# A ring of scores, exponentials over pairs of chunks, and light statistics on ScalarE from tile 5 on

## The chip, the cores and the metric

The kernel runs on one core of a Trainium2 chip. A core has a matrix engine (TensorE, PE in the profile; its weight loads are shown apart as PEld), VectorE (DVE), ScalarE (ACT), GpSimd (POOL) and SyncE (SP, which here only starts DMAs). Each engine takes its own instructions in order, and they wait for one another through semaphores. The metric is the time of one execution on the device in microseconds (us); lower is better.

## The reference

Two layers act on 3327 rows of 256 numbers: a graph convolution, a mixture of experts, a graph attention, and last a causal attention with four heads and four experts in each head. Only the last one is touched. Cut to what matters:

```python
sx = einsum('bsh,ndh->bnsd', x, hl_w) + hl_b            # 4 heads, 64 wide
q = einsum('bnsd,neod->bneso', sx, wq)                  # 4 experts a head
k = einsum('bnsd,nod->bnso', sx, wk); v = einsum('bnsd,nod->bnso', sx, wv)
scores = einsum('bnesd,bntd->bnest', q, k) * d ** 0.5 + causal
qkv = einsum('bnest,bntd->bnesd', softmax(scores), v)
gs = softmax(einsum('bnsf,nef->bnse', out, gate_w) + gate_b)   # gates of the experts
mixed = einsum('bnsed,bnse->bnsd', out, gs)
hn = layernorm(mixed + resid)                           # per head, 64 wide
hx = layernorm(fc2(relu(fc1(hn))) + hn)                 # zeros masked
out = hx * softmax(hx @ fgate_w.T)[..., None] + x
```

Before it, x is normalized over its 256 columns.

## The kernel before

Rows are worked in 26 tiles of 128. `heads` (line 925) is the last stage and runs from about 970 us to the end. Its unit of work is a head of a tile (104 units, in order of tiles). As the attention is causal, tile t has t + 1 key tiles; `span` (1097) cuts them into t // 4 + 1 chunks of at most 512 keys, so units of tiles 0-3 have one chunk, of 4-7 two, of 24 and 25 seven: 392 chunks in all, numbered through in `chunks` (1508).

A chunk goes through these steps, all four experts at once:

- `fill` (1104), TensorE: the scores `pqk` of 128 queries by up to 512 keys, one PSUM bank for each expert. PSUM buffers of the tag "b" are four, and the other small matmuls share them.
- `drain` (1119), VectorE: each expert's scores are copied to `sc` in SBUF, and the largest of each row is kept (the last chunk of a unit adds the causal mask). After the unit's last chunk, one reduction makes `anmax`, the negated maximum.
- `weigh` (1145), ScalarE: `exp(sc - max)` in place, one activation for each expert and chunk, whose accumulated row sum goes to the table `den` at the chunk's own column.
- `turn` (1166), VectorE: one transpose by 32 x 32 blocks of all four experts.
- `attend` (1180), TensorE: the product with the values `vr`, which come from DRAM (`values`, 1159) through SP's queue, summed over the unit's chunks in `po`.

After a unit's last chunk, `over` (1199) copies `po` to `ot` by ScalarE, where POOL multiplies with the padding mask; `back` (1219), one iteration later, turns it with TensorE (`ptO`) and ScalarE copies the result to `qkv`. After a tile's fourth head, `tail` (1326) follows for the tile: gates, mixing, norms, two small linear layers, the final gate, the store. `prepare` (977) and `heads_of` (1026) make the next tile's norm, projections, keys and queries. Tails and preparations are generators that advance one step per iteration of the main loop.

The order on each engine is written out by hand: `InOrder` (50) makes every engine issue in the order of the program. In iteration k of the main loop (1565) the order is: drain until `wanted(k)`; attend chunk k; transpose up to chunk k + 2 (k + 1 where `extra` is 0); load values for k + 2; `weigh` for chunk k + 3 (k + 2), for its first two experts; `back` of the unit that ended before; `over` of the one that ends now; a step of preparations and tails (left out in iterations with a `back`, from tile 8 on); `weigh` for the other two experts; the activations that tails left in `lazy`; the next `fill`. For a unit's first chunk all four experts are weighed after `back`, `over`, preparations and tails. `wanted` (1550) lets drains run so far ahead that the whole unit of the chunk to be weighed is drained. `extra` (1545) is 1 for tiles 5 to 23.

The scores `sc` live in nine rotating buffers of the pool `ats` (932), 512 columns for each expert. The queries of the first five tiles, `qts`, take buffers of that pool too.

`LIGHT` (1086) is 16. Tiles below it take some statistics by VectorE: in `prepare` bn_stats instead of two accumulating activations, in `norm4` (1293) one reduction instead of four accumulating copies, and as the gates' softmax `softmax4` (1273) instead of `weights` (1247), whose sums come with the exponentials and whose reciprocals are powers on POOL. `empty` (949) gives copies out of PSUM to ScalarE or VectorE by a running count of the load of each.

Of the kernel before, what the change touches and what calls it, by code (L numbers as in the profile page):

```python
# [12 lines left out]
F32 = mybir.dt.float32  # L13
# [9 lines left out]
P = 128  # L23
# [5 lines left out]
BLK = 512  # L29
# [72 lines left out]
class Net:  # L102
# [822 lines left out]
    def heads(self, xs, vs, out):  # L925
        tc, a = self.tc, self.a
        nc = InOrder(tc)
        Q = 32
        with ExitStack() as ctx:
            one = ctx.enter_context(tc.tile_pool(name="at", bufs=1))  # L930
            self.work = ctx.enter_context(tc.tile_pool(name="atw", bufs=2))
            scp = ctx.enter_context(tc.tile_pool(name="ats", bufs=9))
            vrp = ctx.enter_context(tc.tile_pool(name="atv", bufs=3))
            tl = ctx.enter_context(tc.tile_pool(name="att", bufs=2))
            sm = ctx.enter_context(tc.tile_pool(name="atsm", bufs=4))
# [5 lines left out]
            )  # L941

            kt = one.tile([P, 4, NP], F32, name="kt")


            load = dict(act=0.0, dve=0.0)
# [78 lines left out]

            def heads_of(t, res, sxt, nz=None, v=None):

                if nz is None:
                    nz = self.work.tile([P, 2, P], F32, tag="xn", name="nz", bufs=1)
                    nonzero(nz, sxt)  # L1030
# [17 lines left out]
                yield  # L1048
                if t < AHEAD:

                    qt = scp.tile([P, 4, BLK], F32, tag="sc", name="qts")[:, :, : 2 * P]
                    qt = qt.rearrange("p h (i q) -> p h i q", i=2)
                else:
                    qt = tl.tile([P, 4, 2, P], F32, tag="qt", name="qt")
# [28 lines left out]

            tails, preps, ready = [], [], {}
            AHEAD = 5
            LIGHT = 16

            def later(n, gen):

# [7 lines left out]
            def span(t, g):  # L1097


                n = t // 4 + 1  # L1100
                lo, hi = (t + 1) * g // n, (t + 1) * (g + 1) // n
                return lo, hi - lo
# [15 lines left out]

            def drain(u, g):

                n = span(u["t"], g)[1] * P
                last = g == u["t"] // 4
                if g == 0:
                    u["sc"] = {}
                    u["mx"] = sm.tile([P, 4, 8], F32, tag="mx", name="mx")
                sc = u["sc"][g] = scp.tile([P, 4, BLK], F32, tag="sc", name="sc")
                for e in range(4):
                    s, m = u["pq"][e][:, :n], u["mx"][:, e, g : g + 1]
                    if last:
                        nc.vector.tensor_tensor_reduce(  # L1130
                            sc[:, e, :n], s, mask[:, BLK - n :], 1.0, NEG, ALU.add, ALU.max, m
                        )
                    else:
                        nc.vector.tensor_scalar(
                            sc[:, e, :n], s, 1.0, None, ALU.mult, ALU.max, accum_out=m
                        )
                    load["dve"] += 0.12 + 0.00104 * n
                if last:
                    u["nmax"] = sm.tile([P, 4], F32, tag="nmax", name="anmax")
                    nc.vector.tensor_reduce(  # L1140
                        u["nmax"], u["mx"][:, :, : g + 1], AX.X, ALU.max, negate=True
                    )
                    load["dve"] += 0.2

            def weigh(u, g, experts):

                n = span(u["t"], g)[1] * P
                q = ready[u["t"]]
                if u["h"] == g == 0 and 0 in experts:
                    q["den"] = sm.tile([P, 16, 7], F32, tag="den", name="aden", bufs=3)  # L1150
                for k in experts:
                    e = u["sc"][g][:, k, :n]
                    nc.scalar.activation(
                        e, e, AF.Exp, bias=u["nmax"][:, k : k + 1],
                        accum_out=q["den"][:, 4 * u["h"] + k, g : g + 1],
                    )
                    load["act"] += 0.26 + 0.00088 * n
# [8 lines left out]
            def turn(u, g):  # L1166


                n = span(u["t"], g)[1] * P
                w = u["sc"][g][:, :, :n]  # L1170
                nc.vector.transpose(w, w)
                load["dve"] += 0.1 + 0.00417 * n

# [331 lines left out]
                nc.sync.dma_start(out=out[ts(t, P), :], in_=fo)  # L1505

            units = [dict(t=t, h=h) for t in range(NT) for h in range(4)]
            chunks = [(u, g) for u in units for g in range(u["t"] // 4 + 1)]
            def begin(u):

                t = u["t"]
# [33 lines left out]
            def extra(k):  # L1545

                t = chunks[min(k + 3, len(chunks) - 1)][0]["t"]
                return int(chunks[k][0]["t"] >= 5 and t // 4 + 1 <= 6)
# [9 lines left out]
            drain_to(wanted(0))  # L1558
            for k in range(2):
                values(*chunks[k])  # L1560
                weigh(*chunks[k], range(4))
            turn(*chunks[0])
            fill_next()
            ended, flipped, weighed = None, 1, 2
            for k, (u, g) in enumerate(chunks):
                drain_to(wanted(k))
                attend(u, g)
# [3 lines left out]
                if k + 2 < len(chunks):  # L1571
                    values(*chunks[k + 2])
                rest = []
                while weighed < min(k + 3 + extra(k), len(chunks)):
                    c = chunks[weighed]
                    if c[1]:
                        weigh(*c, range(2))
                    rest.append((*c, range(2 if c[1] else 0, 4)))
                    weighed += 1
                if ended:  # L1580
                    back(ended)
                last = u if g == u["t"] // 4 else None
# [568 lines left out]
```

## Time and profile before

| | |
|---|---|
| Runs | 2841.45, 2846.56, 2846.6 us, median 2846.56 |
| The profiled execution | 2842.88 us, its span 2840.9 us |
| Granted TensorE clock | 0.98 of full speed |
| Heads stage | about 970 to 2841 us |
| Transposes in it | 392, 816.1 us of VectorE, all sizes |
| Exponentials in it | 1568, 1041.4 us of ScalarE without their accumulator reads |

A profile line names an engine, an operation, what it writes and reads (`sc<-pqk`), the shape, and how often. In grouped views the busy time comes first, then the mean of one in ns, then the idle time of the engine just before such instructions and who ended it. In the timeline each row is a start, a duration, an engine and an operation, and in brackets the idle time before it. All instructions carry line 61, which is the helper that keeps them in order, so they are told apart by the tiles they touch. A scalar accumulation shows as two rows, the activation and ACTIVATION_READ_ACCUMULATOR, and neighbours overlap; the distance between starts is what one costs in a row. TensorE shows each of these matmuls as two records.

### The profile page before, as it was taken

To read this page: it belongs to the slowest core of one execution; us is meant where nothing else is said; L and a number is where in the kernel's file an instruction comes from. 1 tells how busy PE (TensorE), PEld (TensorE's weight loads), DVE (VectorE), ACT (ScalarE), POOL (GpSimd) and SP (SyncE) were. 2 spreads that over 40 slices of the span, in tenths; PEclk is the share of its full clock that TensorE was granted. 3 is DMA by queue.
4 is the path that set the end of the run, shared out by engine and by line. 5 is a ranking of instruction groups with operands and counts; after the bars stand their busy time and mean duration, and the time that the engine had idled before them with its cause. 6 is when DMAs were issued, how large, how long until landed. Compare 5 with 4: busy or idle time off the path is not lost.

```text
span 2840.9 us, 124987 instructions
## 1 busy us (share of the span) xinstructions
PE 2653.9 (93%) x53422; PEld 1970.7 (69%) x53422; DVE 2372.1 (83%) x5521; ACT 1790.9 (63%) x5131; POOL 1077.6 (38%) x1565
## 2 busy tenths in 40 slices
PE   7999988878988998999999999999999999999995
PEld 5888887756767776676666666666666666666664
DVE  5202643589999798999999999999999999999996
ACT  6520135555555467877777777777778777776774
POOL 5541644532133148655444333333233322223122
PEclk9999999989999899999999999999999999999998
DMA  9994568656785333434434443444434434444432
GB/s 379 386 339 138 191 212 281 202 188 238 277 285 174 94 91 88 117 109 112 119 108 117 118 116 114 119 120 121 115 115 116 126 116 124 123 117 117 116 106 80
DMA packets 257755, 449.29 MB, mean 158 GB/s; under 512 B 58768, under 2 KB 156176, under 8 KB 257072
## 3 DMA queue, kind: packets, MB, share of 16 engines
q1 hardware_dynamic: 245104, 417.11, 47.0%
q0 software_dynamic: 6576, 18.02, 1.7%
q8 instruction: 420, 6.88, 1.0%
q10 hardware_dynamic: 5520, 6.18, 0.6%
q14 instruction: 135, 1.11, 0.1%
HBM read 392.98 MB, written 25.88 MB: 147 GB/s over the span
## 4 chain that ended last, share of the span: by engine, by line
DVE 35%; PE 30%; ACT 4%; issue 2%; POOL 1%; DMA 0%; POOLq 0%; DVEq 0%; ACTq 0%
DVE sc L61 32%; PE pqk L61 11%; PE po L61 10%; PE acc L61 3%; ACT sc L61 2%; PE ptO L61 2%; PE pq L61 1%; PE psxt L61 1%; DVE p L61 1%; PE ph L61 0%; PE pk L61 0%; PE pt L61 0%; DVE sg L61 0%; ACT sq L61 0%; DVE u L61 0%
## 5 line engine op out<-in xcount | busy, mean ns | idle before, releaser
L61 ACT ACTIVATE sc<-sc,anmax 128x512 f32<-128x512 f32 (+3 forms) x1568 | 1041.4, 669 | 101.9 <-DVE anmax L61 101.8
L61 PEld LDWEIGHTS po<-sc,vr 32*64 32x64 f32 x43728 | 659.2, 131 | 300.9 <-issue 149.1
L61 DVE STREAM_TRANSPOSE sc<-sc 128x2048 f32<-128x2048 f32 (+3 forms) x392 | 816.1, 2082 | 11.7 <-ACT sc L61 11.5
L61 PE MATMUL po<-sc,vr 32*64 32x128 f32 x43728 | 758.8, 275 | 32.4 <-DVE sc L61 18.2
L61 PE MATMUL pqk<-kt,qt 64*128 64x512 f32 (+1 forms) x2944 | 764.8, 586 | 19.4 <-DVE fgs L61 7.1
L61 DVE TENSOR_SCALAR_CACHE_REDUCE sc<-pqk 128x512 f32<-128x512 f32 (+2 forms) x1152 | 653.3, 621 | 28.7 <-PE pqk L61 26.7
L61 PEld LDWEIGHTS pqk<-kt,qt 64*128 64x128 f32 x2944 | 315.0, 186 | 240.7 <-issue 85.5
L61 PE MATMUL acc<-wh,p 128*128 128x259 f32 x1352 | 310.9, 387 | 35.3 <-DVE p L61 35.2
L61 PEld LDWEIGHTS acc<-wh,p 128*128 128x128 f32 x1352 | 254.0, 191 | 92.2 <-DVE p L61 51.9
L61 PE MATMUL acc<-y,pan 128*128 128x256 f32 x1352 | 298.4, 382 | 1.7 <-issue 1.7
L61 ACT ACTIVATION_READ_ACCUMULATOR sc<-sc,anmax 128x1 f32 x1568 | 299.5, 191 | 0.0
L61 PEld LDWEIGHTS acc<-y,pan 128*128 128x128 f32 x1352 | 257.2, 191 | 38.7 <-issue 3.3
L61 POOL TENSOR_TENSOR ot<-ot,sxd 128x512 f32<-128x512 f32 x83 | 105.8, 1275 | 435.9 <-ACT ot L61 435.9
L61 DVE CUSTOM_DVE_ANT_0 sc<-pqk,mask 128x512 f32<-128x512 f32 (+3 forms) x416 | 242.0, 636 | 21.1 <-PE pqk L61 20.8
L61 ACT ACTIVATE u<-u,d 128x512 f32<-128x512 f32 (+1 forms) x182 | 125.1, 688 | 156.4 <-DVE u L61 156.2
L61 DVE SCALAR_TENSOR_TENSOR p<-pan,u 128x512 f32<-128x512 f32 (+1 forms) x182 | 127.7, 702 | 11.7 <-PE acc L61 7.3
L61 DVE SCALAR_TENSOR_TENSOR u<-bc,d 128x512 f32<-128x512 f32 (+1 forms) x182 | 136.3, 749 | 0.1
L61 PE MATMUL ptO<-igw,ot 128*128 128x68 f32 x832 | 116.1, 283 | 4.3 <-DVE sc L61 2.1
L61 ACT COPY qkv<-ptO 128x272 f32<-128x272 f32 x104 | 39.7, 382 | 126.7 <-PE ptO L61 126.6
L61 PEld LDWEIGHTS ptO<-igw,ot 128*128 128x128 f32 x832 | 101.8, 193 | 23.1 <-issue 15.2
L61 ACT ACTIVATE junk<-ar 128x1664 bf16<-128x1664 f32 x52 | 82.8, 1592 | 54.3 <-DMA ar<-in_adj_dram 53.7
L61 DVE CUSTOM_DVE_ANT_0 sg<-sg,dst 128x1664 bf16<-128x1664 bf16 (+2 forms) x56 | 100.7, 1806 | 1.2 <-ACT dst L61 1.0
(366 smaller groups left out, 3074.6 us busy)
## 6 DMA issues: line engine op xcount, KB each, us to landing
vr<-vs SPq DMA_DIRECT2D x976, 128.0 KB
ar<-in_adj_dram SPq DMA_DIRECT2D x104, 832.0 KB
vr<-vs SPq DMA_DIRECT2D x544, 96.0 KB
pan<-in_adjt_dram SPq DMA_DIRECT2D x156, 256.0 KB
pan<-in_adjt_dram SPq DMA_DIRECT2D x26, 1024.0 KB
pan<-in_adjt_dram SPq DMA_DIRECT2D x20, 832.0 KB
w1e<-w SPq DMA_DIRECT2D x59, 256.0 KB
took<-places SPq DMA_DIRECT2D x59, 129.0 KB
```

What stands on the lines that cost most here:

```text
L61: made = make(*args, **kw)
```

## The change

The nine buffers become one tile `ring` of nine slots, with the column of a chunk worked out by hand (six slots for the 24 chunks of tiles 0-4, whose queries lie in the last three). Where an even chunk that is not the unit's last has the next slot beside it (`paired`), it is put at the end of its slot, so that it and the next chunk lie side by side, and one activation for each expert takes the exponential of both and leaves one sum; the second column of `den` is then never written, so the table is zeroed by POOL in `heads_of`, with four buffers instead of three. `weigh` takes the number of a chunk. In the main loop a pair that does not begin a unit is split over two iterations, two experts in each; a pair that begins a unit is weighed whole, after `back`, `over`, preparations and tails. `LIGHT` becomes 5. The lines of the steps `fill`, `attend`, `values`, `turn`, `extra` and `wanted` stay as they are but for the place of the scores.

```diff
@@ -929,7 +929,6 @@
         with ExitStack() as ctx:
             one = ctx.enter_context(tc.tile_pool(name="at", bufs=1))
             self.work = ctx.enter_context(tc.tile_pool(name="atw", bufs=2))
-            scp = ctx.enter_context(tc.tile_pool(name="ats", bufs=9))
             vrp = ctx.enter_context(tc.tile_pool(name="atv", bufs=3))
             tl = ctx.enter_context(tc.tile_pool(name="att", bufs=2))
             sm = ctx.enter_context(tc.tile_pool(name="atsm", bufs=4))
@@ -941,6 +940,10 @@
             )
 
             kt = one.tile([P, 4, NP], F32, name="kt")
+
+
+            RING = 9
+            ring = one.tile([P, 4, RING * BLK], F32, name="ring")
 
 
             load = dict(act=0.0, dve=0.0)
@@ -1025,6 +1028,9 @@
 
             def heads_of(t, res, sxt, nz=None, v=None):
 
+                den = sm.tile([P, 16, 7], F32, tag="den", name="aden", bufs=4)
+                nc.gpsimd.memset(den, 0.0)
+                res.update(den=den)
                 if nz is None:
                     nz = self.work.tile([P, 2, P], F32, tag="xn", name="nz", bufs=1)
                     nonzero(nz, sxt)
@@ -1048,7 +1054,7 @@
                 yield
                 if t < AHEAD:
 
-                    qt = scp.tile([P, 4, BLK], F32, tag="sc", name="qts")[:, :, : 2 * P]
+                    qt = ring[:, :, ds(6 * BLK + 2 * P * t, 2 * P)]
                     qt = qt.rearrange("p h (i q) -> p h i q", i=2)
                 else:
                     qt = tl.tile([P, 4, 2, P], F32, tag="qt", name="qt")
@@ -1083,7 +1089,7 @@
 
             tails, preps, ready = [], [], {}
             AHEAD = 5
-            LIGHT = 16
+            LIGHT = 5
 
             def later(n, gen):
 
@@ -1118,12 +1124,15 @@
 
             def drain(u, g):
 
+                c = u["c"] + g
                 n = span(u["t"], g)[1] * P
+                at = slot(c) * BLK + (BLK - n if paired(c) else 0)
                 last = g == u["t"] // 4
                 if g == 0:
-                    u["sc"] = {}
+                    u["sc"], u["at"] = {}, {}
                     u["mx"] = sm.tile([P, 4, 8], F32, tag="mx", name="mx")
-                sc = u["sc"][g] = scp.tile([P, 4, BLK], F32, tag="sc", name="sc")
+                sc = u["sc"][g] = ring[:, :, ds(at, n)]
+                u["at"][g] = at
                 for e in range(4):
                     s, m = u["pq"][e][:, :n], u["mx"][:, e, g : g + 1]
                     if last:
@@ -1142,14 +1151,24 @@
                     )
                     load["dve"] += 0.2
 
-            def weigh(u, g, experts):
-
+            def slot(c):
+
+                return c % (RING if c >= 24 else 6)
+
+            def paired(c):
+
+                u, g = chunks[c]
+                return g % 2 == 0 and g < u["t"] // 4 and slot(c) + 1 == slot(c + 1)
+
+            def weigh(c, experts):
+
+                u, g = chunks[c]
                 n = span(u["t"], g)[1] * P
+                if paired(c):
+                    n += span(u["t"], g + 1)[1] * P
                 q = ready[u["t"]]
-                if u["h"] == g == 0 and 0 in experts:
-                    q["den"] = sm.tile([P, 16, 7], F32, tag="den", name="aden", bufs=3)
                 for k in experts:
-                    e = u["sc"][g][:, k, :n]
+                    e = ring[:, k, ds(u["at"][g], n)]
                     nc.scalar.activation(
                         e, e, AF.Exp, bias=u["nmax"][:, k : k + 1],
                         accum_out=q["den"][:, 4 * u["h"] + k, g : g + 1],
@@ -1167,7 +1186,7 @@
 
 
                 n = span(u["t"], g)[1] * P
-                w = u["sc"][g][:, :, :n]
+                w = u["sc"][g]
                 nc.vector.transpose(w, w)
                 load["dve"] += 0.1 + 0.00417 * n
 
@@ -1505,7 +1524,11 @@
                 nc.sync.dma_start(out=out[ts(t, P), :], in_=fo)
 
             units = [dict(t=t, h=h) for t in range(NT) for h in range(4)]
-            chunks = [(u, g) for u in units for g in range(u["t"] // 4 + 1)]
+            chunks = []
+            for u in units:
+                u["c"] = len(chunks)
+                chunks += [(u, g) for g in range(u["t"] // 4 + 1)]
+
             def begin(u):
 
                 t = u["t"]
@@ -1558,10 +1581,10 @@
             drain_to(wanted(0))
             for k in range(2):
                 values(*chunks[k])
-                weigh(*chunks[k], range(4))
+                weigh(k, range(4))
             turn(*chunks[0])
             fill_next()
-            ended, flipped, weighed = None, 1, 2
+            ended, flipped, weighed, begun = None, 1, 2, 0
             for k, (u, g) in enumerate(chunks):
                 drain_to(wanted(k))
                 attend(u, g)
@@ -1571,12 +1594,21 @@
                 if k + 2 < len(chunks):
                     values(*chunks[k + 2])
                 rest = []
-                while weighed < min(k + 3 + extra(k), len(chunks)):
-                    c = chunks[weighed]
-                    if c[1]:
-                        weigh(*c, range(2))
-                    rest.append((*c, range(2 if c[1] else 0, 4)))
-                    weighed += 1
+                until = min(k + 3 + extra(k), len(chunks))
+                while weighed < until:
+                    left = range(begun, 4)
+                    if chunks[weighed][1]:
+                        half = len(left) // 2
+                        weigh(weighed, left[:half])
+                        left = left[half:]
+                    rest.append((weighed, left))
+                    weighed += 2 if paired(weighed) else 1
+                    begun = 0
+                if weighed < len(chunks) and chunks[weighed][1] and paired(weighed) and not begun:
+                    if not rest or rest[0][1][0] > 1:
+                        weigh(weighed, range(1))
+                        rest.append((weighed, range(1, 2)))
+                        begun = 2
                 if ended:
                     back(ended)
                 last = u if g == u["t"] // 4 else None
```

## The prediction

> **What bounds the kernel now.** I read the page first, then the busy times by stretch, the chain of waits, VectorE's waits, and the timeline around single units. The page's busy shares and the chain that ended last:
>
> ```profile
> PE 2653.9 (93%) x53422; PEld 1970.7 (69%) x53422; DVE 2372.1 (83%) x5521; ACT 1790.9 (63%) x5131; POOL 1077.6 (38%) x1565
> ...
> DVE 35%; PE 30%; ACT 4%; issue 2%; POOL 1%; DMA 0%; POOLq 0%; DVEq 0%; ACTq 0%
> ```
>
> VectorE and TensorE share the end; ScalarE carries 4% of the chain. The shares are means, so here are the stretches of the heads stage: tiles 5-7, 8-11, 12-15, 16-23, 24-25 (a tile starts with its first transpose). Columns: window, length, then busy us and instructions of PE, weight loads, DVE, ACT, POOL.
>
> ```profile
> 1102.00:1229.90 127.90, 124.04 (x2944) 88.33 (x2928) 116.54 (x299) 96.72 (x309) 89.03 (x123) 0.99 0.38 108
> 1229.90:1460.10 230.20, 226.09 (x5908) 157.56 (x5914) 218.50 (x531) 173.69 (x546) 115.05 (x155) 1.00 0.40 113
> 1460.10:1762.10 302.00, 295.19 (x8138) 203.57 (x8130) 292.11 (x670) 222.55 (x689) 120.25 (x165) 0.99 0.41 116
> 1762.10:2571.10 809.00, 797.00 (x22870) 539.50 (x22861) 794.17 (x1710) 610.19 (x1934) 243.79 (x336) 1.00 0.41 119
> 2571.10:2841.00 269.90, 222.44 (x7030) 150.80 (x7013) 243.97 (x539) 177.19 (x565) 62.55 (x86) 0.97 0.36 104
> ```
>
> VectorE is busy 91, 95, 97 and 98% in the first four. TensorE's figure holds stalls inside its matmuls, so I take its floor from unstalled pieces of the chain: scores of a chunk 1.49 us (384 wide) or 1.92 (512), its attention 1.58 or 2.02, 1.04 per unit for the way back, some 6.15 per tile for projections and tail. Tile 10 (chunks 384, 512, 512): 4 x (5.33 + 5.62 + 1.04) + 6.15 = 54.1 us, against 56.9 of VectorE. So VectorE sets the pace from tile 8, by a little at first, alone from tile 12. Its waits from 1100 to 2700 us:
>
> ```profile
> DVE sc L61 <- PE pqk L61: 38.2, 45, 4.9
> DVE sc L61 <- ACT sc L61: 0.9, 3, 0.4
> ```
>
> It almost never waits for exponentials: 0.9 us. That is the cover the change draws on. One unit (tile 20, head 3):
>
> ```profile
> 2206.90 0.18 DVE L61 TENSOR_REDUCE anmax<-mx 128x4 f32<-128x24 f32 x1
> 2207.00 2.30 DVE L61 STREAM_TRANSPOSE sc<-sc 128x2048 f32<-128x2048 f32 x1
> 2207.12 0.62 ACT L61 ACTIVATE sc<-sc,anmax 128x384 f32<-128x384 f32 x1 [2.62 <-DVE anmax L61]
> ...
> 2208.93 0.60 ACT L61 ACTIVATE sc<-sc,anmax 128x384 f32<-128x384 f32 x1
> ...
> 2209.44 0.18 ACT L61 ACTIVATION_READ_ACCUMULATOR sc<-sc,anmax 128x1 f32 x1
> 2209.53 0.70 ACT L61 ACTIVATE sc<-sc,anmax 128x512 f32<-128x512 f32 x1
> ...
> 2211.11 1.77 DVE L61 STREAM_TRANSPOSE sc<-sc 128x1536 f32<-128x1536 f32 x1
> ```
>
> The exponentials of a unit's first chunk cannot start before its maximum (2207.08), and VectorE comes to their transpose 4.03 us later, after one other transpose and one drain. Four exponentials of 384 take 4 x 0.60 = 2.41; they are done at 2209.62, so 1.49 us are spare.
>
> **The change, part by part.** *Paired exponentials.* Starts are 0.60 us apart at 384 columns and 0.705 at 512, so 0.00082 us per column and 0.28 fixed. A pair drops one fixed part for each of four experts. Of 168 candidate pairs in tiles 4-25 the ring's wrap cuts 18: 150 x 4 x 0.28 = 168 us less ScalarE work. But all four double exponentials of a unit's first pair stand before the first transpose. In the unit shown, 4 x 1.02 (896 columns) = 4.08, plus the 0.12 that the last read and the signal take: 2207.12 + 4.20 = 2211.32 against 2211.11, a new wait of 0.21 us on VectorE. Queued behind it are that transpose and the next chunk's drain, whose score banks TensorE's next fill wants; the attention of the chunk itself comes two iterations later and has slack.
>
> The wait is larger where the start is late:
>
> ```profile
> 2128.07 0.37 ACT L61 COPY xt<-pt 128x256 f32<-128x256 f32 x1 [8.90 <-PE pt L61]
> 2128.34 0.62 ACT L61 ACTIVATE sc<-sc,anmax 128x384 f32<-128x384 f32 x1
> ```
>
> Here (tile 20, head 0) a copy of the next tile's preparation, in line before the exponentials, waited for TensorE, and they started 2.5 us after the maximum. The change leaves that order. I took start and transpose of all 81 units whose first chunk pairs and put in the longer exponentials (1.02 us at 896 columns, 1.13 at 1024, less for shorter): waits add up to 2.5 us in tile 4, 6.1 in 5-7, 11.6 in 8-11, 6.5 in 12-15, 15.1 in 16-23, 4.0 in 24-25, 45.8 in all. Were every start immediate (0.03 us after the maximum), it would be 11.5. These are the two bounds. Late starts come mostly from TensorE's order, which stays, so I keep the upper one but count 0.8 of the 25.6 from tile 12 on (VectorE's chain; some of its waits for scores shrink in return) and 0.4 of the 20.2 before (TensorE nearly equal): 20.5 + 8.1 = **+28.6**.
>
> The row and a page differ here. The Trainium skill (ScalarE: Activation LUTs, What ACT_TABLE_LOAD costs) gives 280 ns + 0.833 per column, with 93 ns of overlap back to back, and names no accumulator read; by it four of 896 would last 3.73 us, and the 0.21 above would vanish, the change coming out as in the first rival. The 0.60 and 0.705 measured here include the accumulator read, and I go by them.
>
> *Statistics from tile 5 on.* VectorE loses, per tile, by its rows: the sums l1ns and l2ns 0.32 + 0.30, bn_stats, aggregate and epsilon 0.32 + 0.19 + 0.15, and in the gates a subtraction, two sums and two reciprocals, 0.17 + 0.15 + 0.12 + 0.18 + 0.16; with 0.02 between dependent ones some 2.25 us, 24.7 over 11 tiles. It counts until TensorE's floor: in 5-7 the floors sum to 115.1 against 116.5, so 1.4; in 8-11 209.5 against 218.5, all 9.0; in 12-15 all 9.0. That is 19.4 at best; two nearly equal engines never meet exactly, so **-17** (bounds -10, -19.4). ScalarE gains per tile eight sums at 0.36, four gate exponentials at 0.28 for one of 0.2, and two statistics of some 0.5 and 0.6: 5.0 us, 55 in all. From tile 16 on these run today, and the xres reader there shows no idle before it, so the load is not late. In 5-7, with 10 pairs, ScalarE grows by 15 - 11.3 = 3.7 on 96.7 of 127.9 us. That is room on the mean; bursts can still hold a copy that TensorE wants. Bounds 0 and +6, taken **+1**, as tiles 16-23 carry the same bursts with VectorE at 98%. POOL gains two powers (1.02, 0.57) and two small multiplies, 2.0 us a tile, with 39 us idle in 5-7; without that room it would be 22 us.
>
> A rule speaks against this part: the same page (Rules for kernel authors) sends additions to VectorE, not ScalarE. The rows agree on cost, 0.32 against 4 x 0.36; by the rule the 55 us given to ScalarE outweigh 24.7 and the part would lose some 30 us. It would where ScalarE was the bound, which the stretches deny.
>
> *Less ScalarE work elsewhere.* 168 - 55 = 113 us net. The chain holds ScalarE for 4%, mostly bursts before a copy that TensorE's next fill wants; what can come back is part of the 38.2 us above. Bounds 0 and -10, taken **-4**.
>
> *Ring, zeroed sums, query tiles.* No DMA moves. A slot is nine chunks behind from chunk 24, as the buffers were; earlier six serve where a drain runs at most four ahead. The transposes already step over gaps (1.77 us for 384 columns, 2.30 for 512: the slope of the data alone). The zeroing is one POOL write per tile; the nearest row, 256 columns, takes 1.08 us, 26 x 1.08 = 28 us at most, all inside POOL's idle time and a tile ahead of its reader. **0** for all; if a slot were late on the first tiles, some 2 us.
>
> Sum: 28.6 - 17 + 1 - 4 = **+8.6 us**. The profiled execution took 2842.88 us (span 2840.9 and 2 around it), 3.7 under the median of the runs, 2846.56; on the median it makes 2855, on the profile 2851. I say **2854**.
>
> **Rivals.** *VectorE's relief wins.* If ScalarE, with 113 us less to do, is ready at each maximum, the wait is 11.5 at most, about 8 exposed: 8 - 17 - 4 = -13, 2834. For it: three units in four from tile 16 start within 0.1 us already. Against it: the late ones wait for TensorE. It decides below an exposed wait of 15 us. *They cancel.* With about 20 us exposed the sum is 0: 2847. *ScalarE's bursts become the bound in tiles 5-15.* There VectorE's relief is worth nothing and each of 11 tiles loses 2 us more behind the sums: 8.6 + 17 + 22 = +48, 2894; half of it 2870. Against it, the mean load under 80%. *The ring does not do what it says*: if slices of the one tile were taken to overlap, each of the 150 pairs would hold back a drain of another slot, at 1 us each +150. The key table kt is one tile written and read by slices today, and its writes wait only for their own matmuls.
>
> **How the numbers follow.** Slower by the unit's wait 0.38 (own range 2849 to 2866); relief wins 0.32; cancel 0.17; bursts 0.11; ring 0.02. A measurement of this kernel tells about 0.2%, 5.7 us, from no change. Faster 0.32, same 0.17, slower 0.51. The range 2831 to 2876 leaves out the low end of the relief and the high end of the bursts.
>
> **What would show it.** VectorE's waits for "ACT sc" grow from 0.9 to 20-45 us, at first transposes of units; ScalarE's exponentials fall by 600, its busy time by 100 us or so; tiles 16-25 become 10 to 18 us longer and 5-15 a few us shorter or equal. Wrong, if those waits stay under 10 us, or if tiles 16-25 keep their length.

## The result and the profile after

The changed kernel takes 2911.88 us in the median (2907.19 to 2917.77, five runs), the kernel before 2846.60 beside it (2841.45 to 2849.00): 1.023 times as long, 95% interval 1.0214 to 1.0246, or 65 us more. The prediction said 2854 with a range up to 2876: the right direction, an eighth of the size.

The page of the changed kernel, busy shares and the chain that ended last:

```profile
PE 2683.9 (92%) x53422; PEld 1984.8 (68%) x53422; DVE 2357.5 (81%) x5411; ACT 1671.6 (57%) x4239; POOL 1104.1 (38%) x1635
...
PE 28%; DVE 24%; ACT 15%; POOL 3%; issue 2%; SPq 1%; DMA 0%; POOLq 0%; DVEq 0%; ACTq 0%
```

ScalarE works 119 us less than before (1790.9) and yet its share of the chain goes from 4% to 15%. VectorE, 15 us less busy, falls from 35% to 24%. Work became less and waiting became more. The same stretches as before, by tiles 5-7, 8-11, 12-15, 16-23, 24-25 (window, length, then busy us and instructions of PE, weight loads, DVE, ACT, POOL):

```profile
1103.80:1240.80 137.00, 125.91 (x2900) 89.59 (x2902) 113.74 (x280) 93.35 (x274) 92.44 (x133) 0.98 0.36 101
1240.80:1484.80 244.00, 231.11 (x5932) 159.83 (x5931) 211.69 (x489) 176.27 (x542) 119.65 (x168) 0.99 0.38 106
1484.80:1798.60 313.80, 301.49 (x8118) 202.82 (x8116) 286.52 (x634) 207.56 (x572) 134.82 (x193) 0.99 0.40 112
1798.60:2634.00 835.40, 809.02 (x22874) 545.73 (x22870) 795.03 (x1698) 535.67 (x1399) 247.55 (x347) 0.99 0.41 115
2634.00:2910.00 276.00, 224.69 (x6970) 152.67 (x6962) 244.60 (x537) 151.81 (x397) 62.77 (x87) 0.95 0.36 101
```

They are longer by 9.1, 13.8, 11.8, 26.4 and 6.1 us: about half of the loss lies in tiles 5-15, where the prediction had "a few us shorter or equal"; tiles 16-25 lose 32.5 us where it had 10 to 18. In tiles 16-23 VectorE does the same work (795.0 us against 794.2) in 26.4 us more. VectorE's waits from 1100 to 2770 us (us in total, times, longest):

```profile
DVE ring L61 <- PE pqk L61: 66.3, 66, 6.2
DVE ring L61 <- ACT ring L61: 50.6, 61, 2.1
```

The wait for exponentials grew from 0.9 to 50.6 us; that for scores from 38.2 to 66.3, of which the prediction expected some to shrink. (Its other signs came: 600 exponentials fewer and some 100 us less of ScalarE; the wait was put at 20 to 45.) The unit shown of before (tile 20, head 3), in the timeline of after:

```profile
2262.43 0.18 DVE L61 TENSOR_REDUCE anmax<-mx 128x4 f32<-128x24 f32 x1
2262.52 2.30 DVE L61 STREAM_TRANSPOSE ring<-ring 128x2048 f32<-128x2048 f32 x1
2262.64 1.04 ACT L61 ACTIVATE ring<-ring,anmax 128x896 f32<-128x896 f32 x1 [4.04 <-DVE anmax L61]
...
2265.73 1.03 ACT L61 ACTIVATE ring<-ring,anmax 128x896 f32<-128x896 f32 x1
...
2266.67 0.19 ACT L61 ACTIVATION_READ_ACCUMULATOR ring<-ring,anmax 128x1 f32 x1
...
2266.89 1.78 DVE L61 STREAM_TRANSPOSE ring<-ring 128x1536 f32<-128x1536 f32 x1 [0.17 <-ACT ring L61]
```

Four exponentials 1.03 us apart, 4.25 us from the first start to the transpose, and a wait of 0.17 us: the prediction worked out 0.21 for this unit. So the picture of the wait is right. What it is worth, and what else was lost, is what the experiments are for.

### The profile page after: what moved, and what is told of

Its sections match the earlier page's. It is cut to its first block, busy times and chain, and to the rows that moved or that the text cites. A ratio compares the mean times of both kernels' runs of the same rounds, so it can differ in the third digit from the quotient of the medians.

```text
span 2910.0 us, 124041 instructions
## 1 busy us (share of the span) xinstructions
PE 2683.9 (92%) x53422; PEld 1984.8 (68%) x53422; DVE 2357.5 (81%) x5411; ACT 1671.6 (57%) x4239; POOL 1104.1 (38%) x1635
## 4 chain that ended last, share of the span: by engine, by line
PE 28%; DVE 24%; ACT 15%; POOL 3%; issue 2%; SPq 1%; DMA 0%; POOLq 0%; DVEq 0%; ACTq 0%
DVE ring L61 21%; ACT ring L61 11%; PE po L61 10%; PE pqk L61 9%; PE acc L61 4%; PE ptO L61 2%; ACT sq L61 1%; POOL fx L61 1%; PE pq L61 1%; SPq L61 1%; PE psxt L61 1%; PE ph L61 1%; DVE p L61 0%; PE pt L61 0%; DVE sg L61 0%
## 5 line engine op out<-in xcount | busy, mean ns | idle before, releaser
L61 ACT ACTIVATE ring<-ring,anmax 128x896 f32<-128x896 f32 (+7 forms) x968 | 873.5, 907 | 146.4 <-DVE anmax L61 146.3
L61 PEld LDWEIGHTS po<-ring,vr 32*64 32x64 f32 x43728 | 670.9, 132 | 301.1 <-issue 132.5
L61 DVE STREAM_TRANSPOSE ring<-ring 128x2048 f32<-128x2048 f32 (+3 forms) x392 | 816.2, 2083 | 66.8 <-ACT ring L61 66.3
L61 PE MATMUL pqk<-kt,qt 64*128 64x512 f32 (+1 forms) x2944 | 779.1, 589 | 51.9 <-ACT qt L61 11.5
L61 PE MATMUL po<-ring,vr 32*64 32x128 f32 x43728 | 770.3, 278 | 31.1 <-DVE ring L61 17.9
L61 DVE TENSOR_SCALAR_CACHE_REDUCE ring<-pqk 128x512 f32<-128x512 f32 (+2 forms) x1152 | 653.8, 621 | 47.5 <-PE pqk L61 46.1
L61 PE MATMUL acc<-wh,p 128*128 128x259 f32 x1352 | 309.9, 386 | 36.5 <-DVE p L61 36.4
L61 DVE CUSTOM_DVE_ANT_0 ring<-pqk,mask 128x512 f32<-128x512 f32 (+3 forms) x416 | 242.2, 636 | 33.1 <-PE pqk L61 32.7
L61 ACT ACTIVATION_READ_ACCUMULATOR ring<-ring,anmax 128x1 f32 x968 | 185.2, 191 | 0.0
L61 PEld LDWEIGHTS ptO<-igw,ot 128*128 128x128 f32 x832 | 102.1, 193 | 30.4 <-issue 13.0
```

The source lines that it names most:

```text
L61: made = make(*args, **kw)
```

## The experiments

Edits are against the changed kernel unless "before" is said, and all of these but late_first_light put `LIGHT` back to 16. "Whole" means that the block of the main loop that begins a pair an iteration early is taken out:

```diff
-                if weighed < len(chunks) and chunks[weighed][1] and paired(weighed) and not begun:
-                    if not rest or rest[0][1][0] > 1:
-                        weigh(weighed, range(1))
-                        rest.append((weighed, range(1, 2)))
-                        begun = 2
```

Medians in us, each beside the kernel before on the same chip; the waits between 1100 and 2750 us are VectorE's for exponentials and for scores (before: 0.9 and 38.2, to 2700) and, last, TensorE's for ScalarE's other work, nearly all copies, summed over its tiles (before: 5.1). The waits are those of the profiled execution; for odd_pairs that is its shortest run (2884.1), for odd_whole its longest (2870.2).

| run | this | before | ratio, 95% interval | waits: ACT, PE pqk | TensorE for ACT |
|---|---|---|---|---|---|
| ring_only | 2846.91 | 2845.85 | 0.9997 (0.9986 to 1.0008) | 0.6, 38.8 | 5.1 |
| pairs_only | 2899.07 | 2845.85 | 1.0190 (1.0168 to 1.0212) | 36.5, 47.7 | 22.3 |
| light_only | 2857.46 | 2845.85 | 1.0044 (1.0029 to 1.0058) | 2.1, 65.2 | 15.3 |
| odd_pairs | 2895.27 | 2845.85 | 1.0176 (1.0159 to 1.0193) | 9.2, 63.3 | 38.5 |
| odd_whole | 2859.58 | 2849.65 | 1.0036 (1.0022 to 1.0051) | 3.3, 50.9 | 10.6 |
| even2_whole | 2857.23 | 2849.65 | 1.0029 (1.0018 to 1.0040) | 2.6, 40.2 | 9.8 |
| even_whole | 2880.51 | 2843.76 | 1.0115 (1.0078 to 1.0151) | 37.2, 34.7 | 8.0 |
| first_only | 2882.95 | 2843.76 | 1.0132 (1.0096 to 1.0168) | 36.6, 35.7 | 7.9 |
| half_first | 2854.53 | 2848.55 | 1.0028 (1.0015 to 1.0040) | 5.0, 36.9 | 8.2 |
| single_in_turn | 2984.03 | 2848.64 | 1.0488 (1.0458 to 1.0518) | 2.3, 146.4 | 87.5 |
| odd_over_first | 2876.89 | 2849.65 | 1.0104 (1.0087 to 1.0121) | 25.0, 35.3 | 12.4 |
| before_over_first | 2847.24 | 2849.65 | 0.9997 (0.9983 to 1.0011) | 3.2, 36.6 | 2.8 |
| late_turn | 2897.33 | 2848.64 | 1.0175 (1.0150 to 1.0199) | 2.1, 71.3 | 14.6 |
| late_first | 2888.16 | 2847.33 | 1.0148 (1.0131 to 1.0165) | 1.6, 62.8 | 5.6 |
| late_first_light | 2898.07 | 2847.33 | 1.0174 (1.0157 to 1.0191) | 2.9, 93.8 | 14.2 |
| light_sums | 2855.61 | 2848.64 | 1.0023 (1.0010 to 1.0036) | 0.6, 48.4 | 9.9 |
| light_rest | 2850.05 | 2848.64 | 1.0006 (0.9996 to 1.0015) | 0.8, 55.7 | 9.6 |
| light_26 | 2868.53 | 2848.55 | 1.0076 (1.0063 to 1.0090) | 0.6, 37.3 | 3.5 |

### The parts alone

The ring and the zeroed table without pairs (ring_only), with pairs (pairs_only), and the statistics in the kernel before (light_only):

```diff
ring_only:
-                return g % 2 == 0 and g < u["t"] // 4 and slot(c) + 1 == slot(c + 1)
+                return False and g < u["t"] // 4 and slot(c) + 1 == slot(c + 1)
light_only, before:
-            LIGHT = 16
+            LIGHT = 5
```

> The changed kernel without any pair and with LIGHT back at 16: ring, zeroed table and query tiles alone. First-pair theory (pairs that begin a unit cost the time) and statistics theory (light statistics from tile 5 on cost it): both say as before, 2847 within 4 us, VectorE's waits for exponentials near 1 us. Ring theory (slices of one tile wait for one another): well above 2847, 2870 or more.

> The changed kernel with LIGHT back at 16: ring and pairs. First-pair theory: tiles 16-25 keep the 33 us that the changed kernel is longer there, tiles 4-15 add some 15 more of waits for the first pair, so 2885 to 2900, and with the relief that the statistics were meant to give missing even 2912 or more. Statistics theory: only the 33 us of tiles 16-25 remain, 2880. Ring theory: as the ring alone.

> The kernel before with LIGHT at 5, nothing else. By the recorded step (VectorE's relief counts): 2847 - 17 + 1 = 2831. Statistics theory: slower, 2847 + 15 to 35 = 2862 to 2882, all of it in tiles 5-15, with ScalarE and POOL in the chain there.

The ring costs nothing. Pairs cost 53 us and the statistics 12; together 65, the whole loss: as far as these runs can tell, the two add up. The statistics, from which the prediction hoped for 17 us of gain, lose, though less than the 15 to 35 us of the rival expectation.

### Which pairs cost

If the wait at a unit's first transpose is the cause, pairs that start at the second chunk should be free (odd_pairs). They were not: the excess is 49 us, more than either expectation had (6 at most, or 0.7 of 53):

```diff
-                return g % 2 == 0 and g < u["t"] // 4 and slot(c) + 1 == slot(c + 1)
+                return g % 2 == 1 and g < u["t"] // 4 and slot(c) + 1 == slot(c + 1)
```

> LIGHT 16, and pairs begin at odd chunks (1 and 2, 3 and 4, 5 and 6), so a unit's first chunk is never paired; some 107 pairs remain of 150. First-pair theory: VectorE's waits for exponentials fall back to a few us and the time to 2847 within 6 us, lower if anything. If pairs cost wherever they stand (longer single instructions ahead of the copies): 0.7 of what pairs_only loses.

VectorE's wait for exponentials is almost gone (9.2 us), but its wait for scores stands at 63.3, and TensorE waits for ScalarE's copies (12.2 us for `ot`, 5.6 for `sxt`, 4.7 for `sx`). So there is a second cost, which does not come from first pairs. The suspicion fell on the pairs that are begun early. By the kernel's loop, of the 69 pairs of the change that do not begin a unit 53 are begun one iteration before a single chunk in their place would be, and 16 two or three; of the 113 pairs of odd_pairs 45 are begun early, 41 of them by two. odd_whole takes that away; even2_whole has only the pairs (2, 3) and (4, 5), whole; even_whole all the pairs of the change, whole; first_only the first pair of each unit alone:

```diff
even2_whole:
-                return g % 2 == 0 and g < u["t"] // 4 and slot(c) + 1 == slot(c + 1)
+                return g % 2 == 0 and g and g < u["t"] // 4 and slot(c) + 1 == slot(c + 1)
first_only:
-                return g % 2 == 0 and g < u["t"] // 4 and slot(c) + 1 == slot(c + 1)
+                return g == 0 and g < u["t"] // 4 and slot(c) + 1 == slot(c + 1)
```

> odd_pairs without the splitting of a pair over two iterations. Queue theory: what costs, beside the wait at a first transpose, is the time of exponentials that ScalarE has in line between a unit's maximum and the copy of the previous unit's sums (ot), which TensorE's next attention waits for. Per unit of tiles 16-23, at 512 columns: before 4 + 4 + 2 singles = 7.1 us; odd_pairs 4 singles, 4 and 1 doubles = 8.5; single_in_turn 8 + 4 + 2 singles = 9.9. Here 4 singles and 4 doubles = 7.3, so most of the 29 us that odd_pairs loses in tiles 16-23 comes back: 2850 to 2862. If longer single instructions cost by themselves, it stays at 2885 or more.

> Pairs only from chunk 2 on (2 and 3, 4 and 5), not split over iterations. Queue theory: 4 + 4 singles and 2 doubles stand before ot = 8.0 us, 0.9 more than before, in all units from tile 12: slower than odd_whole, 2865 to 2885. If only first pairs and split pairs cost: 2847 within 6.

> pairs_only without the splitting of pairs over two iterations: first pairs stay. If the splitting is what costs (odd_pairs fell from +50 to +10 without it), 2855 to 2865. If first pairs cost their wait whole, 36 us by VectorE's waits in pairs_only, on top of the 8 that whole pairs from chunk 2 on cost: 2885 to 2893, and the waits for exponentials stay at 30 to 40 us.

> Only the 81 first pairs, chunks 0 and 1, whole; all later chunks single. Wait theory: the 36 to 41 us of waits remain and are all exposed, 2880 to 2890. If they hide in other idle time (the recorded prediction counted 0.4 of them in tiles 4-11 and 0.8 later), 2847 + 8 + 17 = 2872 or less; if splitting alone costs, 2847 within 6.

Each beside its own kernel before, whole pairs cost 39 us less than begun ones in odd_whole (10 against 49), and 16 us less in even_whole (37 against 53; by the ratios 21, give or take 12): beginning a pair early costs that much. TensorE's waits for ScalarE's copies go the same way, from 38.5 to 10.6 us and from 22.3 to 8.0. Pairs later in a unit, kept whole, cost 8 to 10 us (even2_whole, odd_whole; less for the former than the queue theory expected). First pairs alone cost 39 us, all pairs whole 37, which falls between the two expectations for even_whole. In first_only that stands beside a wait of 36.6 us that the kernel before did not have, with VectorE's wait for scores nearly unchanged.

Two numbers alike are no proof that the wait is the cost; late_first, below, takes the wait away and gains nothing. So half_first shortens the wait and leaves the order as it is: in first_only, the first chunk's transpose is done in two halves of two experts, the first of which needs only two of the four exponentials.

```diff
-                nc.vector.transpose(w, w)
+                for h in range(2 if not g and paired(u["c"]) else 1):
+                    x = w[:, ds(2 * h, 2), :] if not g and paired(u["c"]) else w
+                    nc.vector.transpose(x, x)
```

> Only the first pairs of units, whole, as in first_only (36.6 us of VectorE waits for ScalarE, +37 us, about 2883), and the transpose of a paired first chunk is done in two halves of two experts, 81 transposes more. By the slope of the rows (1.77 us for 384 columns, 2.30 for 512) a half costs about 0.2 us of fixed part, so VectorE gets about 16 us more work. Theory: the wait of VectorE for the last of the four double exponentials is itself the cost. The second half is due 1.1 us later than the whole transpose was, most of the 53 waits of 0.7 us mean vanish: waits for ScalarE under 12 us, time 2883 - 28 + 16 = about 2871 (2862 to 2877). Rival: the wait is only where VectorE happens to stand when something else is late (scores, copies); then the waits for ScalarE fall but those for TensorE grow by as much, and the time is 2883 to 2899.

VectorE's waits of first_only, and then of half_first:

```profile
DVE ring L61 <- ACT ring L61: 36.6, 53, 2.1
DVE ring L61 <- PE pqk L61: 35.7, 35, 6.2
```

```profile
DVE ring L61 <- PE pqk L61: 36.9, 42, 6.2
DVE ring L61 <- ACT ring L61: 5.0, 12, 0.9
```

31.6 us of the wait are gone and did not turn up at the scores; the profiled spans went from 2879.3 to 2852.9 us, 26.4 less. The 1.0132 of the first pairs becomes 1.0028, and 2854.5 us is below the 2862 to 2877 expected, because the halves cost less than the 16 us put in for them: 59 chunks of 384 columns take 110.0 us in halves and 104.6 (59 at 1.773) whole, and VectorE's busy time grows by 4.0 us in all. With these, 30.4 of the 31.6 us are accounted for. That the wait for the last of the four exponentials was the price of the first pairs is shown.

### The order on ScalarE

single_in_turn keeps the places and the times at which pairs_only issues a pair, but issues it as eight single exponentials, chunk by chunk; work and instructions are those of ring_only:

```diff
-                n = span(u["t"], g)[1] * P
-                if paired(c):
-                    n += span(u["t"], g + 1)[1] * P
+                for i in range(2 if paired(c) else 1):
+                    u, g = chunks[c + i]
+                    n = span(u["t"], g)[1] * P
...
```

> LIGHT 16, the places and the order of the pairs, but each pair as eight single exponentials, the first chunk's four ahead of the second's. ScalarE has the 170 us more again, and the same clumping, but a unit's first chunk is ready as early as before. Turn theory (the loss of pairs_only, some 53 us, is VectorE standing at the first transpose, 41 us by its trace): VectorE's waits for exponentials fall under 10 us and the time to 2855, within 8. Copy theory (exponentials done earlier than needed stand before the copies that free score banks): 2885 or more, above all in tiles 16-25.

It takes some 135 us more than ring_only for the same instructions in another order: VectorE waits 2.3 us for exponentials, but 146 for scores, and TensorE 87.5 us for ScalarE's copies. A piece of its chain of waits (start, length, engine and tile, pieces joined):

```profile
2005.69 5.32 ACT ring L61 x16
2011.02 0.25 ACT sq L61 x2
...
2012.40 1.41 ACT ring L61 x4
2013.81 0.52 ACT sxt L61 x2
2014.32 0.04 issue
2014.37 1.25 PE pqk L61 x2
2015.62 3.40 PE po L61 x116
```

Here both chunks' exponentials of a unit's first pair (16 rows with their accumulator reads) run first, though the second chunk's are wanted later; then statistics, two exponentials of the next pair, begun early, and only then the copy `sxt`, for which the next scores wait. The chain of the changed kernel has a place of the same kind:

```profile
2007.74 1.08 ACT qt L61 x2
2008.82 0.26 ACT fot L61
2009.09 4.09 ACT ring L61 x8
2013.18 1.12 ACT gss L61 x8
2014.30 1.13 ACT ring L61 x2
2015.43 0.27 ACT sx L61
2015.69 0.04 issue
2015.74 1.31 PE pqk L61 x4
```

Its timeline (cut) names the blocks:

```profile
2008.96 1.06 ACT L61 ACTIVATE ring<-ring,anmax 128x896 f32<-128x896 f32 x1
...
2012.00 0.44 PE L61 MATMUL pt<-ident,sxt 128*128 128x128 f32 x2
...
2014.20 1.14 ACT L61 ACTIVATE ring<-ring,anmax 128x1024 f32<-128x1024 f32 x1
...
2015.74 1.31 PE L61 MATMUL pqk<-kt,qt 64*128 64x512 f32 x4 [1.89 <-ACT sx L61]
```

The copy `sx` of 0.27 us stands behind 6.34 us of exponentials and gate sums: the four of a unit's first pair (896 columns each), the gates' `gss`, and one of 1024 columns, the first expert of the next pair, begun an iteration early. What it copies came from TensorE at 2012.00 to 2012.44, and TensorE waited 1.89 us for it. A doubled exponential is cheaper as a sum, but it is a longer block in a line that is worked in order.

If copies are what suffers, they may go first. odd_over_first puts all exponentials of an iteration behind the copies of `back` and `over` and of preparations and tails; before_over_first does it in the kernel before:

```diff
before_over_first, before:
-                    if c[1]:
-                        weigh(*c, range(2))
-                    rest.append((*c, range(2 if c[1] else 0, 4)))
+                    rest.append((*c, range(4)))
```

> odd_pairs, split as there, but no exponential is issued before the copies qkv and ot of its own iteration; all come after. Queue theory: the double that stood before ot is behind it, 7.3 us again, so 2850 to 2865. If the copies of preparations and tails are what is held, no gain: 2885 or more.

> The kernel before with that order alone: all four exponentials of a chunk after the copies of its iteration. Queue theory: 5.7 us before ot instead of 7.1, so no slower, 2847 within 4, and perhaps some us faster in tiles 5-11. Against it: VectorE's transposes may now wait for the two exponentials that come later, 2850 to 2860.

For the pairs it helps by some 20 us against odd_pairs (27 us over its kernel before, against 49), less than the queue theory expected (2850 to 2865): TensorE's waits for copies fall from 38.5 to 12.4 us and VectorE's for scores from 63.3 to 35.3, but that for exponentials rises from 9.2 to 25.0. The copies' loss is in part handed on to the transposes. Two things changed at once, though: by the loop, the 41 pairs begun two iterations early are here begun only one early, so how much the order alone is worth is not shown. In the kernel before, with single exponentials, the order makes no difference that can be told.

### Transposing later

The first chunk's transpose may come one iteration later, when its exponentials are surely done; late_turn does this for every chunk of tiles 5 to 23, late_first only for first chunks that pair (whole pairs), late_first_light adds `LIGHT` 5:

```diff
late_turn:
-                while flipped < min(k + 2 + extra(k), weighed, len(chunks)):
+                while flipped < min(k + 2, weighed, len(chunks)):
late_first:
+                    if extra(k) and flipped == k + 2 and not chunks[flipped][1] and paired(flipped):
+                        break
```

> LIGHT 16 and all pairs, but transposes run one iteration later in tiles 5-23, so the pair has some 5 us more. Turn theory: VectorE's waits for exponentials in tiles 5-23 fall from 38 to under 5 us; time 2855 within 10, or under 2847 if ScalarE's lighter load then counts. Copy theory: 2885 or more, with the lost time as waits for scores. A third way: TensorE now waits for the late transposes, PE po behind DVE ring, and gives it back.

> even_whole (all pairs, whole, LIGHT 16), only that the transpose of a unit's first chunk is put off by one iteration where it is paired, behind the next drain. Wait theory: the 37 us of waits for exponentials go, the order on ScalarE stays, so 2847 + 0 to 10 us, what whole pairs cost elsewhere; below 2847 only if ScalarE's 170 us less count for anything. If the late transposes hold TensorE, as all late ones did, 2875 or more and PE po waits for DVE ring.

> The same with LIGHT at 5. If the statistics cost 12 us only because ScalarE's line was full, its 170 us less pay for that and VectorE's relief counts: up to 17 us under late_first, so this would be below the kernel before. If the sums stand before the copies all the same: 8 to 14 us over late_first.

None is clearly shorter than its like without the move (late_turn 2897 to pairs_only's 2899, late_first 2888 to even_whole's 2881). The wait theory's times (2855, 2847 to 2857) were missed; what came is the other outcome named, that late transposes hold TensorE. VectorE hardly waits for exponentials any more, but late_turn makes TensorE's attention wait 44.0 us for VectorE's `ring` (9.1 in pairs_only), and late_first makes TensorE wait 17.2 us (`ptO`) and 10.6 (`pqk`) for it (2.0 and 7.8 in even_whole), and VectorE 62.8 for scores. A place in late_first's timeline shows how:

```profile
2167.60 0.69 DVE L61 TENSOR_SCALAR_CACHE_REDUCE ring<-pqk 128x512 f32<-128x512 f32 x1 [2.50 <-PE pqk L61]
...
2170.15 3.97 DVE L61 STREAM_TRANSPOSE ring<-ring 128x1536 f32<-128x1536 f32 x2
```

In the slot that the transpose left, VectorE has nothing to do until scores come (2.50 us); an iteration later it does two transposes in a row (3.97 us), and the drains behind them free the score banks late. With the statistics as well it is another 10 us, within the 8 to 14 expected.

### The statistics

light_sums gives ScalarE only the two norms' sums from tile 5 on, light_rest the other half, gates and the preparation's statistics (both in the kernel before). light_26 goes the other way: all statistics to VectorE up to the last tile.

```diff
light_sums, before (the same for "l2"):
-                yield from norm4(fx, lng, lnb, "l1", t < LIGHT)
+                yield from norm4(fx, lng, lnb, "l1", t < 5)
light_26, before:
-            LIGHT = 16
+            LIGHT = 26
```

> The kernel before, only the two norms' sums by ScalarE from tile 5 on. light_only lost 12 us. Lazy theory (a norm's sums stand in ScalarE's line right before the copy of ptO that TensorE's next scores wait for): most of the loss is here, 2847 + 8 to 14. Statistics-of-rows theory (POOL waits in its order for ScalarE's row statistics and gates, and holds ot back): within 4 us of 2847.

> The kernel before, only the row statistics and the gates moved from tile 5 on, the norms' sums left at 16. It takes 1.6 us of VectorE a tile for 2.1 us of ScalarE. Lazy theory: 2847 or some us less (relief counts: -5 to -10). Statistics-of-rows theory: 2847 + 8 to 12.

> The kernel before with the limit LIGHT at 26 in place of 16: in tiles 16 to 25 the two norms' sums, the gates' sums and reciprocals and the preparation's statistics go to VectorE, which is 98% busy there. By the rows of the prediction 2.25 us of VectorE per tile, 10 tiles: +22 us if VectorE alone sets the pace there (about 2869, tiles 16 to 25 longer by 20 or so). Rival: the end passes to and fro between VectorE and the copies of ScalarE that free score banks, and ScalarE, relieved of 5 us a tile, makes copies sooner: +12 or less (2847 to 2859).

The sums make up some 7 of the 12 us; the rest cannot be told from nothing, though it takes 12 us of work from VectorE, which would have gained time if VectorE set the pace there. A few us of the 12 lie in neither half, or in the noise. The chain of light_only in tile 8 shows their way to the end:

```profile
1228.72 2.39 ACT sc L61 x8
1231.11 0.25 ACT sq L61 x2
...
1233.95 0.44 ACT sq L61 x2
1234.39 1.20 ACT sc L61 x4
1235.59 0.28 ACT qkv L61
1235.86 0.04 issue
1235.91 1.64 PE pqk L61 x2
```

Eight accumulating activations of two norms, 3.3 us, run between the exponentials; the copy `qkv`, 0.28 us, comes last, and TensorE's scores wait for it. Between the starts of tiles 5 and 16 VectorE waits for scores 24.9 us in the kernel before and 47.6 in light_only:

```profile
DVE sc L61 <- PE pqk L61: 24.9, 24, 4.9
```

```profile
DVE sc L61 <- PE pqk L61: 47.6, 57, 4.2
```

VectorE's busy time fell by 18.1 us and its wait for scores rose by 22.7: the relief was turned into waiting. TensorE's waits for ScalarE's copies rose from 5.1 to 15.3 us. light_26 shows that the price itself was right where VectorE alone sets the end: 2.25 us a tile over ten tiles make 22, measured 20 to 22 (1.0076 of 2848.55 is 21.6). There the chain reads

```profile
DVE 42%; PE 25%; issue 2%; ACT 2%; DMA 1%; POOL 1%; SPq 0%; POOLq 0%; DVEq 0%; ACTq 0%
```

with VectorE's share up from 35%. Of the three limits tried, 5, 16 and 26, 16 is the best, and no version here is faster than the kernel before.

## Why the prediction was wrong, by its steps

The prediction fell 56 us short, +8.6 against +65. The step that failed most is the statistics' relief: -16 with its bursts, measured +12, so 28 us. The pairs begun early, at nothing in the sum, are 16; the part of the first-transpose wait that was not counted is 8 or so; the gain from a lighter ScalarE, which did not come, is 4.

| term | predicted | measured |
|---|---|---|
| wait at first transposes | +28.6 | +37 to +39 (even_whole, first_only; 33 to 38 by the ratios) |
| pairs begun early | not in the sum | +16 (pairs_only less even_whole) |
| statistics' relief, with its bursts | -17 + 1 | +12 (light_only) |
| less ScalarE work elsewhere | -4 | no gain: half_first, 90 us of ScalarE less, is 1.0028 |
| ring, zeroing, query tiles | 0 | 0 (ring_only) |

**The wait at first transposes** was seen, and its raw size of 45.8 us was near: 36.5 us in pairs_only, 50.6 in the change, where the statistics delay the exponentials further. What failed is the share of it that was counted, 0.8 from tile 12 on and 0.4 before. The argument was that waits for scores shrink in return, and that TensorE is nearly equal before tile 12. They hardly shrink (35.7 in first_only against 38.7 in the same stretch of before). Practically all of the wait counted, as half_first shows. The reading offered for this, argued and not measured apart: when VectorE waits, the score banks are emptied later too, and two engines that are both nearly full and feed each other through four buffers are not two floors of which the higher one counts.

**The pairs that are split over two iterations** were named in the description of the change and never costed; some are even begun two iterations ahead. That they issue earlier than the single exponentials did was the one thing to see: for every instruction moved forward in an engine's line, ask what it is now in front of. Here it is in front of the copies `ot`, `sx`, `sxt`, `qkv` and `qt`.

**The statistics' relief** was worked out by floors: VectorE's time until TensorE's sum. The size of the edit was right (light_26), but the end in tiles 5-15 does not follow the higher of two floors. The trace of before had shown it: followed stage by stage, its chain gives VectorE 7% in tiles 5-7 and 26% in 8-11, TensorE 69% in both, and VectorE leads only from tile 12 (62%), while the prediction let VectorE set the pace from tile 8. light_rest agrees: 12 us less of VectorE, no time. And the bursts, bounded at 6 us for three tiles because "tiles 16-23 carry the same bursts", cost in tiles 5-15 more than VectorE gained. The rule which the prediction weighed and set aside, that additions belong to VectorE and not to ScalarE (the Trainium skill, ScalarE: Activation LUTs, Rules for kernel authors), had the sign right (light_only, 1.0044). ScalarE was not full, 57 to 64% busy; in the places looked at, what lost was the copies that stood behind the sums in its line. The rival "ScalarE's bursts become the bound in tiles 5-15" had this mechanism, at twice the size for the statistics.

**Less ScalarE work** is the smallest term, but the idea behind the change. 119 us fewer on an engine with idle time gave nothing back that shows, and its share of the chain went up from 4% to 15%. What ScalarE lacked was not time but the right moment.

What stays open: why pairs later in a unit cost 8 to 10 us even when whole (TensorE's waits for copies account for some 5), although with first pairs they add nothing; how the early pairs' 16 us divide between the copies `ot`, `sx`, `sxt`, `qkv` and `qt`; and how late_first's 41 us divide between the emptied slot and the doubled one.

## What to carry to other kernels

Here, fusing small instructions on an engine that works in order and has time to spare saved no time and lengthened the block that stands before the next consumer: before fusing, look at what is waiting for the first half, and what is queued behind the second. A stall between two engines that were both over 90% busy and share few buffers counted in full here, so give no discount on one without a trace that shows the return. If one consumer must wait for a longer block, let it take its input in parts, as the two halves of a transpose did here for 31.6 us of waiting.

## What the runs showed of the hardware that was not expected

TensorE's granted clock fell to half for 3.4 us, at times for 6.8 or 10.2, after stretches in which it did little, and the stalls made by the order on ScalarE were long enough for it. Two neighbouring windows of the changed kernel (length, PE busy and, third from the end, the clock):

```profile
1985.80:1989.20 3.40, 1.90 (x6) 0.33 (x3) 2.93 (x7) 3.37 (x11) 0.93 (x1) 1.00 0.36 108
1989.20:1992.60 3.40, 3.40 (x117) 3.32 (x116) 2.92 (x3) 2.84 (x11) 0.17 (x1) 0.51 0.03 7
```

TensorE was busy 1.90 of 3.40 us, with one idle gap of 1.50 us before scores that waited for the copy `sxt`; in the next 3.40 us it had half the clock, and an attention that takes 2.02 us elsewhere took 3.57. Between 1000 and 2750 us the clock's record has half speed for 13.7 us in the kernel before, 47.8 in the changed one, and 112.6 in single_in_turn. As an estimate, if half the time at half speed is lost, this is at most (47.8 - 13.7) / 2 = 17 us of the 65, and (112.6 - 13.7) / 2 = 49 of single_in_turn's 135. From first_only to half_first it fell from 34.1 to 17.1 us, so up to 8.5 of the 26.4 us won there came by way of the clock, which the stalls had lowered. In the four traces gone through for this (before, after, pairs_only, single_in_turn) every such stretch there followed 3.4 us with at most 2.4 us of TensorE's work, though not every idle stretch was followed by one; in light_only one followed 2.5 us of work. The Trainium skill (TensorE: Matmul & The Clock Gate, HAM oscillation) gives as its rule no idle gaps over some 3.4 us; here a gap of 1.50 us was enough.
